# Statistics, Newton steps and three of four row tiles of the layer norm on GpSimd, in the first stage of a two-layer adaptive-norm kernel

## The chip, the cores and the metric

The kernel runs on one core of one Trainium2 chip, as one launch. The metric is device time in microseconds. A program's several executions are given by their median; the time of an execution is a little longer than the span that the profiler records from its first to its last instruction.

Engines are named as in the profile: PE (TensorE matrix products; PEld its weight loads), DVE (VectorE), ACT (ScalarE), POOL (GpSimd), SP (SyncE, here only issuing transfers). Each engine runs its own instructions in program order and waits on semaphores for the others.

## The reference

Two layers work on `x` of 4 batches x 1024 tokens x 256 features, all in float32. In each, `x` is normalised over its features, scaled and shifted by a modulation, sent through a mixing block, gated and added; the same again with a mixture of experts. The change concerns the two norms of the first layer:

```python
def _layernorm(x, axis=-1, eps=1e-05):
    m = jnp.mean(x, axis=axis, keepdims=True)
    v = jnp.var(x, axis=axis, keepdims=True)
    return (x - m) / jnp.sqrt(v + eps)
...
    x = L0_attn_hidden_states
    mod = (_silu(L0_c) @ L0_wmod).reshape(L0_c.shape[0], 6, 1, -1)
    sa, ca, ga, sb, cb, gb = (mod[:, 0], mod[:, 1], mod[:, 2], mod[:, 3], mod[:, 4], mod[:, 5])
...
    h = _layernorm(x, axis=-1) * (1 + ca) + sa
    x = x + ga * _L0_attn_ref(h, L0_attn_queries, L0_attn_combiners)
    h = _layernorm(x, axis=-1) * (1 + cb) + sb
    x = x + gb * _L0_ffn_ref(h, L0_ffn_W1, L0_ffn_b1, L0_ffn_W2, L0_ffn_b2, L0_ffn_Wr, L0_ffn_br)
...
```

`_L0_attn_ref` is attention without a softmax, in four head groups of 64, so it can be reordered: from the Gram matrix of the normalised tokens, a 64x64 product per group and the combiners, one matrix `md` is made per batch, and the block's output is `h` times `md`. `_L0_ffn_ref` picks the best two of eight experts per token by a router and runs each expert (256 to 1024 to 256). The second layer has a mixing block of gated products and again eight experts of which two are picked.

## The kernel before

**Stages.** The first stage (about the first 95 us) does the norms, the mixing block and the router of layer 0 and writes the normalised rows, with each token's expert numbers, to a table in memory (`h_rows`). Then come blocks of 128 token slots, gathered by expert, through the experts of layer 0; then layer 1. Only the first stage is touched by the change; from the first expert block on, each engine's program order is the same in both kernels.

**Tiles.** A row tile is 128 tokens x 256 features. A batch `b` has eight, taken in two groups `g` of four. For each batch there is a *first half* (`first_half`) and a *second half* (`second_half`), each with two groups, so `normalised` is called for 16 groups, 64 tiles in all.

**The norm of a group** (`normalised`). `stats` (L1097 to L1101) makes a tile's statistics on DVE: `bn_stats` gives six numbers per token (count, mean and sum of squared deviations of even and of odd elements), `bn_aggr` makes mean and variance of them, and after the fourth tile one operation adds epsilon (`ln_v`). `root` (L1105) takes the square root of the four variances on ACT. `newton` (L1109 to L1116) takes the reciprocal, one Newton step and `-mean * y` (`ln_m`) on DVE, each on 128x4 numbers. `scaled` writes the normalised tiles into `xn`: by `by_gpsimd`, tiles 0 and 1 of a group on POOL (L1126) and tiles 2 and 3 on ACT (L1128).

**Behind it.** `to_features` transposes the four tiles on PE (`pm_t`, L1168, 8 products), and ACT scales and shifts them while it takes them out of PSUM (L1173, `h1T` or `h2T`). It starts once all four tiles of the group are normalised. `to_tokens` transposes back (`pm_b`, L1195) and ACT copies the result over `xn` (L1200).

In a first half, PE then makes the Gram matrix from both groups (`pm_gram`, L1256), DVE copies its diagonal blocks (`gd`, L1267), PE multiplies by the combiners (`pm_t1`, L1289; the profile prints `pm_t`) and, after a copy by ACT (L1299), by the queries (`pm_m`, L1311), and DVE multiplies with the gate into `md` (L1324). In a second half, PE makes the block's output (`pm_o`, L1352), DVE adds it to `x` (L1362), two tiles at a time, the norm runs again, and PE makes the router's logits (`pm_e`, L194) and turns them to tokens (`pm_l`, L1404). DVE picks the best two experts in twelve operations (`route`, L420 to L446); SP stores rows and numbers (L1436, L1449). At the end of the stage `pm_turn` (L454 to L456) turns the choices of all tokens, and counting and the first gather by POOL (L353) follow.

**What sets the order.** The order on each engine is written by a list scheduler when the program is built (`Plan`): a piece of work is given by its engine, an assumed duration, the pieces that it follows, the buffers that it holds and a rank; at each planned moment the ready piece of the lowest rank goes to its engine. `FIRSTS` and `SECONDS` are the ranks of the batches' halves. `SPLIT` names the batch whose route is made in two halves of four tiles; the others are routed as eight. Where the plan leaves PE idle, pieces named `busy` (L1033, products of a constant that nobody reads) have been put, at planned times listed in the code and, 12 of them, after the split batch's logits:

```python
    for at in (15.6, 16.2, 16.8, 18.4, 19.0, 19.6, 21.2, 21.8, 23.4, 91.4, 98.9, 99.4):
        kept_busy(0.44, [], 40.0, at)
    for b in range(B):
        first_half(b, [5.5 + 5.0 * b, 8.0 + 5.0 * b])
        second_half(b)
```

**POOL's queue.** Before the norms it holds constants: identity, counters, masks. The mask `below16` (`affine_select`, L304) waits for `same16`, which DVE makes (L302), and behind it lie the clearings of `gd` and `md` and 24 small ones of `g_which` (L578). After the norms it issues the gathers and scatters of the expert blocks. DVE's queue holds, between the norms, the modulation's outputs (`modT`, L1063) and two rows of gates (`gate_of`, L338 to L342).

Of the kernel before, what the change touches and what calls it, by code (L numbers as in the profile page):

```python
# [8 lines left out]
F32 = mybir.dt.float32  # L9
# [3 lines left out]
ALU = mybir.AluOpType  # L13
# [6 lines left out]
P = 128  # L20
B, S, D = 4, 1024, 256
# [6 lines left out]
EPS = 1e-5  # L28
# [117 lines left out]
def adaln_d2_kernel(  # L146
# [20 lines left out]
    nc = tc.nc  # L167
# [36 lines left out]
    x_sb = const.tile([P, NC, B, D], F32, name="x_sb")  # L204
# [10 lines left out]
    pa = poolA.__enter__()  # L215
# [22 lines left out]
    for b in range(B):  # L238
        for g in range(2):
            cs = slice(4 * g, 4 * g + 4)  # L240
# [23 lines left out]
    rank = const.tile([P, E], F32, name="rank")  # L264
# [741 lines left out]
    for name, n in (("ga", 4 * B), ("gb", 3 * B)):  # L1006
        last = (blocks_of(n) - RARE) * P
# [17 lines left out]
    plan = Plan(p1=3, p2=2, pm=3, xn1=5, h1T=2, xn2=6, h2T=2, t1=1, le=2)  # L1025
    PE, ACT, DVE, POOL = "PE", "ACT", "DVE", "POOL"
    tiles = {}
# [56 lines left out]
        )  # L1084

    def by_gpsimd(k, b, g, i):
        return i < 2

    def normalised(b, cs, key, slot, after, rank, at=0.0):

        n = len(cs)

        def stats(c):
            if c == cs[0]:
                tiles["mv", key] = pa.tile([P, n, 2], F32, tag="ln_mv", name="ln_mv", bufs=6)
            st = pa.tile([P, 6], F32, tag="ln_st", name="ln_st", bufs=4)
            nc.vector.bn_stats(st, x_sb[:, c, b, :])  # L1097
            nc.vector.bn_aggr(tiles["mv", key][:, c - cs[0], :], st)
            if c == cs[-1]:
                v = tiles["v", key] = pa.tile([P, n], F32, tag="ln_v", name="ln_v", bufs=6)  # L1100
                nc.vector.tensor_scalar(v, tiles["mv", key][:, :, 1], EPS, None, ALU.add)  # L1101

        def root():
            y = tiles["y", key] = pa.tile([P, n], F32, tag="ln_y", name="ln_y", bufs=6)
            nc.scalar.activation(y, tiles["v", key], AF.Sqrt)  # L1105

        def newton():
            mv, v, y = tiles["mv", key], tiles["v", key], tiles["y", key]
            nc.vector.reciprocal(y, y)  # L1109

            t = pa.tile([P, n], F32, tag="ln_t", name="ln_t")
            nc.vector.scalar_tensor_tensor(t, y, -0.5, y, ALU.mult, ALU.mult)
            nc.vector.tensor_tensor(t, t, v, ALU.mult)
            nc.vector.scalar_tensor_tensor(y, t, 1.5, y, ALU.add, ALU.mult)
            m = tiles["m", key] = pa.tile([P, n], F32, tag="ln_m", name="ln_m", bufs=6)
            nc.vector.scalar_tensor_tensor(m, mv[:, :, 0], -1.0, y, ALU.mult, ALU.mult)  # L1116

        def scaled(i):
            if ("xn", key) not in tiles:
                tiles["xn", key] = pa.tile(  # L1120
                    [P, n, D], F32, tag=slot[0], name=slot[0], bufs=plan.room[slot[0]]
                )
            dst, src = tiles["xn", key][:, i, :], x_sb[:, cs[i], b, :]
            r, m = [tiles[q, key][:, i : i + 1] for q in ("y", "m")]
            if by_gpsimd(*key, i):
                nc.gpsimd.tensor_scalar(dst, src, r, m, ALU.mult, ALU.add)  # L1126
            else:
                nc.scalar.activation(dst, src, AF.Identity, bias=m, scale=r)  # L1128

        last = []  # L1130
        for i, c in enumerate(cs):
            last = [
                plan(
                    DVE,
                    0.54 if i < n - 1 else 0.71,
                    lambda c=c: stats(c),
                    after=[*last, *after(c)],
                    rank=rank,
                    at=at,
                )  # L1140
            ]
        r = plan(ACT, 0.22, root, after=last, rank=rank - 0.2)
        d = plan(DVE, 0.9, newton, after=[r], rank=rank - 0.2)
        done = []
        for i in sorted(range(n), key=lambda i: not by_gpsimd(*key, i)):
            pool = by_gpsimd(*key, i)
            done.append(
                plan(
                    POOL if pool else ACT,
                    0.8 if pool else 0.52,  # L1150
                    lambda i=i: scaled(i),
                    after=[d, *done[:1]],
                    holds=[slot],
                    rank=rank,
                )
            )
        return done
# [57 lines left out]

    of_batch = {}

    FIRSTS, SECONDS, SPLIT = [0, 1.3, 2.42, 2.65], [1.28, 4.7, 2.66, 4.55], 3

    def first_half(b, arrival):  # L1220

# [250 lines left out]
    q = plan("SP", 0.1, gates_out, after=rows_done, rank=-0.8, lag=2.2)  # L1472
# [15 lines left out]
    for half in range(2):  # L1488
# [15 lines left out]
        m = plan(PE, 0.3, turn, after=routes, holds=[ps], rank=rank_)  # L1504
# [38 lines left out]
    d = of_batch["turned"]  # L1543
    m = plan(PE, 0.2, lambda: g0.total_staged(ps_1), after=[d], holds=[ps], rank=-1.0)
# [183 lines left out]
    r, m0 = sought(0, [begun], -1.6)  # L1728
    r, m1 = sought(1, [r], -1.55)
# [11 lines left out]
    m = plan(PE, 0.4, lambda: g0.across(ps_1), after=[closed], holds=[ps], rank=-1.25)  # L1741
    d = plan(DVE, 1.6, lambda: g0.limits(pa), after=[m, bs], holds=[ps], rank=-1.0)
# [106 lines left out]
    def half_turned(j):  # L1849
# [40 lines left out]
        y=3,  # L1890
# [1159 lines left out]
```

## Time and profile before

| | us |
|---|---|
| runs, median of 13 (lowest, highest) | 1079.59 (1076.0, 1081.45) |
| the profiled execution | 1076.4 |
| its span, first to last instruction | 1074.7 |
| busy over the span: PE / PEld / DVE / ACT / POOL | 1037.6 / 802.0 / 602.4 / 396.1 / 425.6 |
| granted PE clock, mean | 0.995 |
| first transpose of the first norm begins (`pm_t`) | 11.91 |
| last `pm_l` of the stage ends | 92.04 |
| second `pm_turn` begins | 94.78 |
| first gather for an expert block (POOL) | 100.63 |

The columns of the views are as follows. A timeline row gives the start and the duration in us, the engine, the line, the operation, the tile written and those read, the shape, and how many instructions are merged. A row by stretches gives the stretch, its length, then the busy time of PE, PEld, DVE, ACT and POOL with the number of instructions, the granted clock, the share of the transfer engines and their rate. Matmuls are pipelined, so their busy time is modelled; the spacing from one start to the next says what one costs when nothing is waited for. On DVE a record starts a little before the record ahead of it ends, so there too the spacing counts. The profiled execution is one of the quicker ones, 3.2 us under the median.

### The profile page before, as it was taken

What the parts mean: (1) busy time and instruction counts of PE and PEld (TensorE: products, weight loads), DVE (VectorE), ACT (ScalarE), POOL (GpSimd) and SP (SyncE); (2) the same over time, 40 slices, a digit from 0 to 9 for tenths busy, and PEclk for the clock granted to TensorE, in tenths of its full rate; (3) what the DMA queues carried; (4) which work ended last, traced back from release to release, by engine and by line L of the source; (5) the groups of instructions that cost most, each with busy time, mean ns of one, the idle gap of its engine ahead of it and who ended that gap; (6) DMA issues with size and microseconds to landing.
All of it is one profiled execution on the core that took longest, in us unless ns stands there. A gap on an engine that the chain in (4) does not pass through costs nothing. (4 is left out here: it accounts for less than half of the span.)

```text
span 1074.7 us, 18875 instructions
## 1 busy us (share of the span) xinstructions
PE 1037.6 (97%) x6193; PEld 802.0 (75%) x6193; DVE 602.4 (56%) x2323; ACT 396.1 (37%) x1077; POOL 425.6 (40%) x509
## 2 busy tenths in 40 slices
PE   8998999999999999999999999999999999998993
PEld 5885899989989989989999465564656566646751
DVE  7997443232222232221175588878778726697767
ACT  5865332323232323232353333422224325342521
POOL 3211466545555655554453010110106321573644
PEclk9999999999999999999999999999999999999997
DMA  8605626675553725464171222221014322352534
GB/s 282 241 21 110 216 62 204 216 273 192 178 167 102 253 64 186 134 212 148 33 267 40 72 59 60 66 82 47 19 34 141 111 66 76 107 169 74 160 112 147
DMA packets 94255, 139.81 MB, mean 130 GB/s; under 512 B 31009, under 2 KB 69933, under 8 KB 89542
## 3 DMA queue, kind: packets, MB, share of 16 engines
q0 software_dynamic: 30080, 68.89, 20.2%
q1 hardware_dynamic: 62966, 68.04, 20.0%
q10 hardware_dynamic: 1104, 1.58, 0.4%
q8 instruction: 53, 0.87, 0.3%
q14 instruction: 52, 0.43, 0.1%
HBM read 202.22 MB, written 29.17 MB: 215 GB/s over the span
## 5 line engine op out<-in xcount | busy, mean ns | idle before, releaser
L1622 ACT ACTIVATE hid<-p_h,w 128x128 f32<-128x128 f32 x504 | 144.0, 369 | 301.4 <-issue 203.6
L1634 PE MATMUL p_y<-w,hid 128*128 128x256 f32 x1008 | 230.5, 382 | 0.6 <-DMA w<-in_W,g_wrow 0.6
L2430 PE MATMUL p_u<-hT,a 128*128 128x512 f32 x512 | 229.3, 595 | 1.3 <-ACTq L2395 0.9
L1634 PEld LDWEIGHTS p_y<-w,hid 128*128 128x128 f32 x1008 | 186.9, 190 | 24.6 <-issue 1.0
L2430 PEld LDWEIGHTS p_u<-hT,a 128*128 128x128 f32 x512 | 94.9, 190 | 103.1 <-issue 92.8
L1610 PEld LDWEIGHTS p_h<-xTq,w 128*128 128x128 f32 x1408 | 163.3, 192 | 1.7
L1610 PE MATMUL p_h<-xTq,w 128*128 128x128 f32 x1408 | 164.5, 275 | 0.0
L353 POOL DMA_INDIRECT w<-in_W,g_wrow x124 | 125.8, 1014 | 67.2 <-ACT hid L1622 42.7
L1645 DVE TENSOR_TENSOR y<-p_y,w 128x256 f32<-128x256 f32 x64 | 27.2, 425 | 193.6 <-PE p_y L1634 190.7
L914 POOL DMA_INDIRECT y<-y,g_dest x64 | 65.9, 1029 | 132.6 <-DVE y L1645 72.5
L2478 PE MATMUL p_f<-a,hf 128*128 128x256 f32 x512 | 116.9, 380 | 0.0
L2478 PEld LDWEIGHTS p_f<-a,hf 128*128 128x128 f32 x512 | 95.9, 190 | 18.7 <-issue 6.4
L2526 POOL TENSOR_TENSOR x_sb<-x_sb,step 128x256 f32<-128x256 f32 x32 | 24.6, 770 | 208.4 <-DVE step L2519 164.6
L860 DVE TENSOR_SCALAR_CACHE_REDUCE g_hits<-pm_counts,g_nth 128x128 f16<-128x128 f32 x68 | 23.7, 348 | 89.4 <-PE pm_counts L847 86.3
L1610 PE MATMUL p_h<-xT,w 128*128 128x128 f32 x608 | 71.3, 276 | 0.4 <-DVE xT L1567 0.4
L1610 PEld LDWEIGHTS p_h<-xT,w 128*128 128x128 f32 x608 | 70.3, 192 | 1.2 <-DVE xT L1567 0.6
L2442 ACT ACTIVATE hf<-p_u,decay 128x512 f32<-128x512 f32 x56 | 38.3, 685 | 77.2 <-PE p_u L2430 73.7
L2738 PE MATMUL p_e<-ew,xT 128*128 x256 | 64.9, 384 | 0.3 <-ACT y L2748 0.3
L2446 DVE SCALAR_TENSOR_TENSOR hf<-p_u,decay,hf 128x512 f32<-128x512 f32 x56 | 41.8, 747 | 22.1 <-PE p_u L2430 10.5
L2089 DVE TENSOR_TENSOR h<-h,mod 128x256 f32<-128x256 f32 x128 | 51.4, 423 | 4.1 <-ACT h L2079 2.1
L353 POOL DMA_INDIRECT xg<-ga_rows,ga_row x36 | 34.2, 950 | 45.6 <-DVE ga_row L869 13.5
L2738 PEld LDWEIGHTS p_e<-ew,xT 128*128 128x128 f32 x256 | 44.8, 190 | 8.6 <-issue 2.9
(420 smaller groups left out, 1340.5 us busy)
## 6 DMA issues: line engine op xcount, KB each, us to landing
yg<-y SPq DMA_DIRECT2D x32, 256.0 KB
xTq<-square SPq DMA_DIRECT2D x176, 32.0 KB
ew<-in_W SPq DMA_DIRECT2D x16, 288.0 KB
ga_y<-y SPq DMA_DIRECT2D x36, 128.0 KB
half<-in_W SPq DMA_DIRECT2D x16, 257.0 KB
x_sb<-in_x SPq DMA_DIRECT2D x8, 512.0 KB
h_rows<-xn SPq DMA_DIRECT2D x8, 512.0 KB
hT<-square SPq DMA_DIRECT2D x128, 32.0 KB
```

The source lines that it names most:

```text
L353: return nc.gpsimd.indirect_dma_start(out=dst, out_offset=None, in_=table, in_offset=bass.IndirectOffsetOnAxis(ap=index, axis=0), bounds_c ...
L914: nc.gpsimd.indirect_dma_start(out=table if parts == 1 else table.rearrange("r (i d) -> (r i) d", i=parts), out_offset=bass.IndirectOffset ...
L1610: nc.tensor.matmul(p1[:, i, :], lhsT=w1[:, k * H + m * P : k * H + (m + 1) * P], rhs=xT[k], start=(k == 0), stop=(k == KD - 1),)
L1622: nc.scalar.activation(hid[:, m, :], p1[:, i, :], AF.Relu, bias=w1buf[j % 2][:, KD * H + m : KD * H + m + 1],)
L1634: nc.tensor.matmul(p2, lhsT=hid[:, m, :], rhs=w2[:, m * D : (m + 1) * D], start=(m == 0), stop=(m == KH - 1),)
L1645: nc.vector.tensor_tensor(y, p2, w2buf[j % 2][:, KH * D :], ALU.add)
L2089: nc.vector.tensor_tensor(h, h, mods1[(sc, sh)[i]][:, b, :], (ALU.mult, ALU.add)[i])
L2430: nc.tensor.matmul(pu, lhsT=a[:, k, m * P : (m + 1) * P], rhs=made["n1", c, "hT"][:, k, :, :], start=(k == 0), stop=(k == KD - 1),)
L2442: nc.scalar.activation(made[key, m], made[key, m, 0], AF.Silu, scale=decays[c])
L2446: nc.vector.scalar_tensor_tensor(h, made[key, m, 1], decays[c], h, ALU.mult, ALU.mult)
L2478: nc.tensor.matmul(made[key, "p2", b], lhsT=made[key, m][:, b * P : (b + 1) * P], rhs=a1[:, m, :], start=(m == 0), stop=(m == KH - 1),)
L2738: nc.tensor.matmul(made[key, "p2"], lhsT=made[key, "xT"][:, k, :], rhs=ew_flat[:, bass.ds(made[key, "at"] + k * D, D)], start=(k == 0), st ...
```

## The change

The aggregation of the statistics leaves DVE. `stats` now only keeps the six numbers of four tiles side by side; a new piece `gathered` on POOL makes the four variances and twice the means of a group in seven operations on 128x4 numbers; the root stays on ACT; the reciprocal alone stays on DVE (`inverse`); the Newton step and `-mean * y` become six operations on POOL. `by_gpsimd` gives POOL three tiles of four. The planner's durations are changed with it, and `FIRSTS`, `SECONDS` and `SPLIT` get new values: the first halves of batches 0 and 1 come first, then the second half of 0, the first halves of 2 and 3, the second halves of 2, 3 and last 1, and batch 2 is the split one. (Before: the second half of 0 stood before the first half of 1 by rank, and the second halves ended with 3 and 1, with 3 split.) The list of `busy` pieces is unchanged.

```diff
@@ -1084,7 +1084,7 @@
         )
 
     def by_gpsimd(k, b, g, i):
-        return i < 2
+        return i < 3
 
     def normalised(b, cs, key, slot, after, rank, at=0.0):
 
@@ -1092,28 +1092,44 @@
 
         def stats(c):
             if c == cs[0]:
-                tiles["mv", key] = pa.tile([P, n, 2], F32, tag="ln_mv", name="ln_mv", bufs=6)
-            st = pa.tile([P, 6], F32, tag="ln_st", name="ln_st", bufs=4)
-            nc.vector.bn_stats(st, x_sb[:, c, b, :])
-            nc.vector.bn_aggr(tiles["mv", key][:, c - cs[0], :], st)
-            if c == cs[-1]:
-                v = tiles["v", key] = pa.tile([P, n], F32, tag="ln_v", name="ln_v", bufs=6)
-                nc.vector.tensor_scalar(v, tiles["mv", key][:, :, 1], EPS, None, ALU.add)
+                tiles["st", key] = pa.tile([P, n, 6], F32, tag="ln_st", name="ln_st", bufs=6)
+            nc.vector.bn_stats(tiles["st", key][:, c - cs[0], :], x_sb[:, c, b, :])
+
+        def gathered():
+            tiles["v", key], tiles["m", key] = [
+                pa.tile([P, n], F32, tag=f"ln_{x}", name=f"ln_{x}", bufs=6) for x in ("v", "m")
+            ]
+            g = nc.gpsimd
+            st, v = tiles["st", key], tiles["v", key]
+            d, q = [
+                pa.tile([P, n], F32, tag=f"ln_{x}", name=f"ln_{x}", bufs=2) for x in ("d", "q")
+            ]
+            g.tensor_tensor(d, st[:, :, 1], st[:, :, 4], ALU.subtract)
+            g.tensor_tensor(d, d, d, ALU.mult)
+            g.tensor_tensor(q, st[:, :, 2], st[:, :, 5], ALU.add)
+            g.tensor_scalar(d, d, 0.25, EPS, ALU.mult, ALU.add)
+            g.tensor_scalar(q, q, 1.0 / D, None, ALU.mult)
+            g.tensor_tensor(v, q, d, ALU.add)
+            m = tiles["m", key]
+            g.tensor_tensor(m, st[:, :, 1], st[:, :, 4], ALU.add)
 
         def root():
             y = tiles["y", key] = pa.tile([P, n], F32, tag="ln_y", name="ln_y", bufs=6)
             nc.scalar.activation(y, tiles["v", key], AF.Sqrt)
 
+        def inverse():
+            nc.vector.reciprocal(tiles["y", key], tiles["y", key])
+
         def newton():
-            mv, v, y = tiles["mv", key], tiles["v", key], tiles["y", key]
-            nc.vector.reciprocal(y, y)
-
-            t = pa.tile([P, n], F32, tag="ln_t", name="ln_t")
-            nc.vector.scalar_tensor_tensor(t, y, -0.5, y, ALU.mult, ALU.mult)
-            nc.vector.tensor_tensor(t, t, v, ALU.mult)
-            nc.vector.scalar_tensor_tensor(y, t, 1.5, y, ALU.add, ALU.mult)
-            m = tiles["m", key] = pa.tile([P, n], F32, tag="ln_m", name="ln_m", bufs=6)
-            nc.vector.scalar_tensor_tensor(m, mv[:, :, 0], -1.0, y, ALU.mult, ALU.mult)
+            v, y, m = tiles["v", key], tiles["y", key], tiles["m", key]
+            t = pa.tile([P, n], F32, tag="ln_t", name="ln_t", bufs=2)
+            g = nc.gpsimd
+            g.tensor_tensor(t, y, y, ALU.mult)
+            g.tensor_tensor(t, t, v, ALU.mult)
+            g.tensor_scalar(t, t, -0.5, 1.5, ALU.mult, ALU.add)
+            g.tensor_tensor(y, t, y, ALU.mult)
+            g.tensor_scalar(m, m, -0.5, None, ALU.mult)
+            g.tensor_tensor(m, m, y, ALU.mult)
 
         def scaled(i):
             if ("xn", key) not in tiles:
@@ -1132,22 +1148,24 @@
             last = [
                 plan(
                     DVE,
-                    0.54 if i < n - 1 else 0.71,
+                    0.42,
                     lambda c=c: stats(c),
                     after=[*last, *after(c)],
                     rank=rank,
                     at=at,
                 )
             ]
+        last = [plan(POOL, 0.75, gathered, after=last, rank=rank - 0.2)]
         r = plan(ACT, 0.22, root, after=last, rank=rank - 0.2)
-        d = plan(DVE, 0.9, newton, after=[r], rank=rank - 0.2)
+        r = plan(DVE, 0.2, inverse, after=[r], rank=rank - 0.2)
+        d = plan(POOL, 0.75, newton, after=[r], rank=rank - 0.2)
         done = []
         for i in sorted(range(n), key=lambda i: not by_gpsimd(*key, i)):
             pool = by_gpsimd(*key, i)
             done.append(
                 plan(
                     POOL if pool else ACT,
-                    0.8 if pool else 0.52,
+                    0.6 if pool else 0.52,
                     lambda i=i: scaled(i),
                     after=[d, *done[:1]],
                     holds=[slot],
@@ -1215,7 +1233,7 @@
 
     of_batch = {}
 
-    FIRSTS, SECONDS, SPLIT = [0, 1.3, 2.42, 2.65], [1.28, 4.7, 2.66, 4.55], 3
+    FIRSTS, SECONDS, SPLIT = [0.4, 0.69, 2.11, 2.24], [1.68, 3.87, 2.33, 2.69], 2
 
     def first_half(b, arrival):
```

## The prediction

> **What bounds the kernel now.** I read the stage table first, because the change lies in the first stage alone (program order on every engine is the same from the first expert block on). Two stretches, from the busy times by stretch (PE, PEld, DVE, ACT, POOL busy us, with instruction counts):
>
> ```profile
> 12.00:30.00 18.00, 16.88 (x176) 12.90 (x176) 16.43 (x70) 12.02 (x24) 3.67 (x7) 1.00 0.89 289
> 30.00:92.00 62.00, 58.74 (x719) 49.59 (x719) 55.62 (x225) 48.05 (x97) 13.10 (x24) 1.00 0.38 122
> ```
>
> The reader is to see that DVE is busy for 72 of these 80 us and POOL for 17, which invites the move, but also that PE is busy for 58.74 of the last 62. Whether that PE time is real I check by spacing, in the timeline:
>
> ```profile
> 36.20 2.09 PE L1256 MATMUL pm_gram<-xn 128*64 128x64 f32 x64
> ...
> 73.92 1.95 PE L1352 MATMUL pm_o<-md,h1T 128*128 128x128 f32 x16
> ```
>
> Back to back, a 128x128 matmul or transpose takes 1.95/16 = 0.122 us and a Gram matmul 2.09/64 = 0.033. The groups by line give 128 `pm_t` + 128 `pm_o` + 128 `pm_b` = 384 x 0.122 = 46.9; 256 Gram = 8.4; 128 router `pm_e` at 0.04 (0.64 for 16) = 5.1; 16 `pm_t1` at 0.257 = 4.1; 64 `pm_m` at 0.043 = 2.8; 8 `pm_l` at 0.11 = 0.9. That is 68.2 us that PE must do after the first transpose. Before, that transpose starts at 11.91 and the last `pm_l` ends at 92.04: 80.1 us, in which PE also does 16 `pm_modT` (1.9), one gate row (1.0) and 20 fillers of 0.213 (4.3). So it idles 4.7 us. PE is the second bound of the stage, right behind DVE, and gives a gain little room.
>
> **The change on DVE and ACT.** The norm's rows on DVE:
>
> ```profile
> 28.08 0.18 DVE L1098 BATCH_NORM_AGGREGATE ln_mv<-ln_st 128x2 f32<-128x6 f32 x1
> 28.18 0.39 DVE L1097 BATCH_NORM_STATS2 ln_st<-x_sb 128x6 f32<-128x256 f32 x1
> 28.61 0.18 DVE L1098 BATCH_NORM_AGGREGATE ln_mv<-ln_st 128x2 f32<-128x6 f32 x1
> 28.82 0.17 DVE L1101 TENSOR_SCALAR ln_v<-ln_mv 128x4 f32<-128x4 f32 x1
> 28.90 0.42 DVE L1097 BATCH_NORM_STATS2 ln_st<-x_sb 128x6 f32<-128x256 f32 x1
> ...
> 37.23 0.14 DVE L1109 RECIPROCAL ln_y<-ln_y 128x4 f32<-128x4 f32 x1
> ...
> 38.00 0.16 DVE L1116 SCALAR_TENSOR_TENSOR ln_m<-ln_mv,ln_y 128x4 f32<-128x4 f32 x1
> 38.08 0.42 DVE L1097 BATCH_NORM_STATS2 ln_st<-x_sb 128x6 f32<-128x256 f32 x1
> ```
>
> A stats-aggregate pair is spaced 0.53. Statistics without the aggregate were never back to back: between 0.32 (the overlap of about 0.08 that rows show) and 0.43 (none). So 64 pairs give back 0.10 to 0.21 each, 6 to 13 us; 16 `ln_v` 0.19 each (28.61 to 28.90, less 0.10), 3.0; and the Newton chain shrinks from 0.85 (37.23 to 38.08) to a reciprocal of 0.20, 16 x 0.65 = 10.4. DVE loses 20 to 27 us of 72. ACT loses 16 tiles of 0.545, 8.7 us of 60. Neither gain reaches the end by itself: PE and POOL come next. The statistics' six columns, now kept for four tiles, cost nothing, as no wait on a statistics buffer shows.
>
> **The change on POOL.** Each of 16 groups gains 7 small operations (aggregate), 6 (Newton) and one tile more. No small two-input operation on POOL is in the trace. The nearest rows:
>
> ```profile
> 2.73 0.18 POOL L289 CAST lane<-lane_i 128x1 f32<-128x1 int32 x1
> 2.85 0.20 POOL L289 CAST twice<-twice_i 128x32 f32<-128x32 int32 x1
> 3.01 0.28 POOL L289 CAST count<-count_i 128x128 f32<-128x128 int32 x1
> ...
> 31.06 0.16 DVE L1116 SCALAR_TENSOR_TENSOR ln_m<-ln_mv,ln_y 128x4 f32<-128x4 f32 x1
> ...
> 31.26 1.09 ACT L1128 ACTIVATE xn<-x_sb,ln_m,ln_y 128x256 f32<-128x256 f32 x2 [0.22 <-DVE ln_m L1116]
> 31.32 1.09 POOL L1126 TENSOR_SCALAR xn<-x_sb,ln_y,ln_m 128x256 f32<-128x256 f32 x2 [6.44 <-DVE ln_m L1116]
> ```
>
> Independent casts are 0.12 to 0.16 apart and take about 0.19. Woken by the same DVE result (ended 31.22), ACT starts 0.04 later and POOL 0.10 later. In the changed program's order, four of the seven and four of the six wait for POOL's own semaphore, so I take 0.19 + 0.10 = 0.29 from one dependent operation to the next and 0.14 between independent ones. Walking the two lists so, the aggregate holds POOL 1.29 us (the variance is out at 1.20), Newton 1.59, and three tiles at 0.545 take 1.64: g = 4.52 us a group, 72.3 in all. Lower end: all thirteen 0.12 apart, g = 3.2 (51 us). Upper end by the farthest row: a small operation as dear as a whole 128x256 tile, 13 x 0.545 + 1.64 = 8.7 a group, 140 us. I take 4.52, as a four-element operation is nearer to the 128x1 cast than to 256 elements; all thirteen in chain at 0.30 would make 5.5.
>
> A rule that speaks against the change stands in the Trainium skill, "GPSIMD Engine Reference", section "Engine selection": elementwise work belongs on VectorE, GpSimd being roughly twice as slow for two-input operations. As an estimate from that page, thirteen operations at twice DVE's spaced 0.20 would make a group 6.8 us, the queue 109 us and the kernel some 40 us slower; no row here shows that.
>
> **When POOL begins.** Its order puts the first aggregate behind `below16` and 24 memsets of `g_which`, which ended at 11.25 before; with six statistics ahead on DVE in place of five pairs I take 11.4. Then 1.20 to the variance, root and reciprocal (0.04 + 0.20 + 0.04 + 0.17 + 0.10), Newton 1.59, one tile, the second group's aggregate, two tiles: the first group is normalised at 17.7, where PE's first transposes started at 11.91. The reciprocal also sits in DVE's order where statistics of later tiles queue behind it, and the root on ACT has the drains of `pm_t` and `pm_b` behind it, whose buffers PE waits for: late POOL holds three queues. At this point DVE and ACT have slack, PE has not.
>
> **The sum by POOL's queue.** 11.4 + 72.3 = 83.7. Four groups (first, eleventh, thirteenth, fifteenth) have Newton straight behind their aggregate: 0.46 us of idling with ACT and DVE free, about 0.9 with half an instruction ahead on each: 3.6. The last first-half group (`xn_965`) must pass transposes, Gram, `t1`, `pm_m`, `pm_o` and the adds before group 13's statistics: 1.05 + 0.78 + 0.60 + 0.59 + 2.09 + 0.59 + 1.03 + 0.59 + 0.69 + 0.59 + 1.06 + 0.69 + 0.69 + 0.42 and a dozen hand-overs of 0.1 = 12.7, against 9.9 of POOL work between: 2.8. So the last tile is out at 90.1. Then the tail:
>
> ```profile
> 87.30 1.08 ACT L1128 ACTIVATE xn<-x_sb,ln_m,ln_y 128x256 f32<-128x256 f32 x2
> ...
> 91.71 0.33 PE L1404 MATMUL pm_l<-ident,le 128*128 128x128 f32 x1
> ...
> 92.08 0.19 DVE L420 TENSOR_REDUCE g_best<-pm_l 128x4 f32<-128x32 f32 x1
> ...
> 94.78 0.23 PE L454 MATMUL pm_turn<-ones,g_both 128*128 128x128 f16 x1 [0.20 <-DVE g_both L446]
> ```
>
> Last tile (88.38) to route 3.7, route to `pm_turn` 2.7. The last route now has eight tiles (batch 1 ends, SPLIT is 2): 3.2, as 86.12 to 89.31 shows; both turns come together, 0.3 more. 90.1 + 3.7 + 3.2 = 97.0, and 0.3: 2.5 us late.
>
> **The sum by PE.** 17.7 + 68.2 + 21 fillers (4.5) + 3 us of starving until batch 1 is normalised = 93.4, against 92.04: 1.4, with 0.8 for route and turns 2.2; if half of the old 4.7 of idling also stays, 4.6. Of 2.5, 2.2 and 4.6 I take 3.5, as two full queues that wait for each other lose more than either alone. On the profiled execution, 1076.4 (its span 1074.7 and 1.7 around it), that is 1079.9; it lay 3.2 under the median of the runs, so I forecast 1079.6 + 3.5 = **1083.1 us**. The stages behind follow one for one.
>
> Another rule would see more room: the Trainium skill, "Perfetto Trace Analysis", section "Identifying the Most-Contended Engine", calls the busy share of weight loads the good metric and the matmul share a bad one. PEld is busy 49.59 of 62, so by that rule, as an estimate from the page, 12 us could go and the kernel reach 1067. The start-to-start spacing says 3.
>
> **Rivals.** A, *PE packs*: POOL's small operations cost the lower end, in the first 25 us and all along. Then the first group is out at 16.0 (1.29 and 1.59 become 0.84 and 0.72), POOL never decides, and PE ends at 16.0 + 68.2 + 4.5 = 88.7 if it never idles otherwise: 2.5 faster after 0.8 for route and turns; at the spacing of weight loads (1.86 us for 16, 0.116) 384 x 0.006 = 2.3 more. 1074.8 to 1077.1, say 1076. For it: DVE 90% busy now. Against: eight waits a group. It decides from g under about 3.6. B, *no change*: g near 4.1, where POOL's sum is 11.4 + 65.6 + 6.4 + 7.2 = 90.6 and only PE's late start is left, against what it packs: within 2 us, 1079.6. C, *the chain is dearer*: g = 5.5, 11.4 + 88 + 6.4 + 7.2 = 113, 18 us late, 1098. Against it: casts of 0.18. D, the code does not do what it says: program order shows the operations on POOL, so no.
>
> **Chances.** Forecast (1081.8 to 1089) 0.47, A 0.25, B 0.17, C and what lies between 0.11. A measurement of this kernel can tell 0.2%, 2.2 us. Faster 0.25, same 0.17, slower 0.58. Range 1074.5 to 1095: A's bound below; above, most of the way to C, with the 8.7 end left out.
>
> **What would show it.** POOL busy about 65 to 75 us of the first 100, small operations 0.25 to 0.30 apart in chains; first `pm_t` at 17 to 18; DVE waiting for ACT's root; `pm_turn` at 97 to 99. If `pm_turn` comes before 92, either POOL's operations were cheaper or my PE count is too high.

## The result and the profile after

The changed kernel took 1095.78 us (median of 8 runs, 1093.59 to 1097.69) against 1079.49 of the kernel before (36 runs, 1076.0 to 1081.46): a ratio of 1.0154, 95% interval 1.0142 to 1.0165, 16.3 us slower. I had forecast 3.5 slower, and a range up to 1095. The direction was right; the size was out by more than a factor of four, and the time lies just outside the range. The profiled execution took 1093.6 us with a span of 1091.6, 16.9 over that of before (1074.7).

The same two stretches as in the prediction, and the end of the stage behind them (busy us of PE, PEld, DVE, ACT, POOL with counts, then the granted PE clock, DMA share and GB/s):

```profile
12.00:30.00 18.00, 12.91 (x118) 9.25 (x119) 11.22 (x39) 7.54 (x16) 14.01 (x64) 0.81 0.89 287
30.00:92.00 62.00, 55.71 (x638) 47.74 (x637) 32.28 (x93) 34.20 (x68) 45.01 (x172) 0.94 0.23 87
92.00:108.00 16.00, 14.47 (x152) 10.08 (x151) 9.96 (x48) 12.69 (x25) 6.38 (x22) 1.00 0.67 157
```

DVE went from 72 to 43.5 us in the first two rows, and POOL from 17 to 59. Over the whole stage (12 to 95 us before, 12 to 108 now) DVE has 74.5 and 53.5 us: 21 less, inside the 20 to 27 that I had worked out. But PE, the second bound, went from 16.88 + 58.74 to 12.91 + 55.71, and part of that at a lower clock: it issued 756 matmuls by 92 us where it had issued 895. No engine is full, and the stage is 13 us longer. So this is a loss by waiting. What waited is in the list of waits between 12 and 108 us (engine, line, what it waited for: us in total, times, longest):

```profile
ACT ln_y L1118 <- POOL ln_v L1112: 23.1, 12, 6.5
DVE ln_y L1121 <- ACT ln_y L1118: 22.4, 10, 5.0
PEld pm_t L1186 <- POOL xn L1142: 9.3, 12, 2.6
ACT xn L1144 <- POOL ln_m L1132: 9.2, 6, 2.5
POOL ln_d L1107 <- DVE ln_st L1096: 8.2, 1, 8.2
```

The first two rows are new and belong to the round trip: ACT stands at the root for POOL's variance, DVE stands at the reciprocal for ACT's root. The last is the other way round, one stall of 8.2 us in which POOL itself has nothing to do.

Was POOL dearer than I had worked out? Its timeline (start, duration, engine, line, operation), one aggregate and one Newton list:

```profile
22.27 0.20 POOL L1107 TENSOR_TENSOR ln_d<-ln_st 128x4 f32<-128x4 f32 x1
22.54 0.20 POOL L1108 TENSOR_TENSOR ln_d<-ln_d 128x4 f32<-128x4 f32 x1
22.69 0.20 POOL L1109 TENSOR_TENSOR ln_q<-ln_st 128x4 f32<-128x4 f32 x1
22.99 0.20 POOL L1110 TENSOR_SCALAR ln_d<-ln_d 128x4 f32<-128x4 f32 x1
23.27 0.22 POOL L1111 TENSOR_SCALAR ln_q<-ln_q 128x4 f32<-128x4 f32 x1
...
23.88 0.20 POOL L1107 TENSOR_TENSOR ln_d<-ln_st 128x4 f32<-128x4 f32 x1
...
43.72 0.20 POOL L1127 TENSOR_TENSOR ln_t<-ln_y 128x4 f32<-128x4 f32 x1
...
45.04 0.20 POOL L1132 TENSOR_TENSOR ln_m<-ln_m,ln_y 128x4 f32<-128x4 f32 x1
45.19 0.20 POOL L1127 TENSOR_TENSOR ln_t<-ln_y 128x4 f32<-128x4 f32 x1
```

A dependent operation follows after 0.27 to 0.28 (L1107 to L1108), an independent one after 0.15 (L1108 to L1109); an aggregate takes 1.61 from start to start (22.27 to 23.88), a Newton list 1.47 (43.72 to 45.19), and 48 tiles lie 0.54 apart. A group is 1.61 + 1.47 + 1.62 = 4.7 us, where I had 4.52. The sum was right to 4%, its parts less so: the aggregate takes 1.61 where I had 1.29, as L1110 and L1111 too start 0.28 to 0.30 after the operation ahead of them, and the Newton list 1.47 (1.63 where a tile follows it, 18.88 to 20.51) where I had 1.59.

How a late POOL list holds three queues is seen best between 40 and 51 us:

```profile
48.49 0.20 POOL L1112 TENSOR_TENSOR ln_v<-ln_q,ln_d 128x4 f32<-128x4 f32 x1
48.64 0.20 POOL L1114 TENSOR_TENSOR ln_m<-ln_st 128x4 f32<-128x4 f32 x1
48.72 0.20 ACT L1118 ACTIVATE ln_y<-ln_v 128x4 f32<-128x4 f32 x1 [6.49 <-POOL ln_v L1112]
48.83 0.56 POOL L1142 TENSOR_SCALAR xn<-x_sb,ln_y,ln_m 128x256 f32<-128x256 f32 x1
48.83 0.57 ACT L1317 COPY t<-pm_t 128x512 f32<-128x512 f32 x1
48.96 0.18 DVE L1121 RECIPROCAL ln_y<-ln_y 128x4 f32<-128x4 f32 x1 [5.00 <-ACT ln_y L1118]
49.17 0.69 DVE L1380 TENSOR_TENSOR x_sb<-x_sb,pm_o 128x512 f32<-128x512 f32 x1
...
49.45 1.12 PE L1329 MATMUL pm_m<-t,qT 128*64 128x64 f32 x16 [3.29 <-ACT t L1317]
```

The planner put the root of one group ahead of the copy of `t` of batch 1 on ACT, and the reciprocal ahead of the adds on DVE. POOL's variance came 6.5 us after ACT stood ready; the copy, whose input PE had finished at 45.3, had to stand behind it, and `pm_m`, the heart of batch 1, stood on PE for the copy. Those are three queues held by one late list. Batch 1 pays (PE's `pm_o` show that the second halves run in the order 0, 1, 2, 3, although batch 1 has the last rank), as PE's and POOL's timelines show further on:

```profile
50.51 5.21 PE L1186 MATMUL pm_t<-ident,xn 128*128 128x128 f32 x20
...
57.94 1.06 PE L1370 MATMUL pm_o<-md,h1T 128*128 128x128 f32 x8
...
63.54 1.06 PE L1370 MATMUL pm_o<-md,h1T 128*128 128x128 f32 x8
```

```profile
68.85 0.20 POOL L1107 TENSOR_TENSOR ln_d<-ln_st 128x4 f32<-128x4 f32 x1 [8.19 <-DVE ln_st L1096]
```

Behind `pm_m` come twenty transposes and batch 0's router; only then `pm_o` of batch 1, whose second part is out at 64.6, and the add and the statistics after it. The add begins at 65.81 only, behind batch 0's route on DVE (62.87 to 65.89), and the statistics have the `gd` copies and another add between them. The eleventh group, the first half of batch 1's second norm, needs them: POOL, which was late at 48, is starved from 60.66 to 68.85.

And the tail, PE's last rows of the stage:

```profile
104.35 0.33 PE L1422 MATMUL pm_l<-ident,le 128*128 128x128 f32 x1
...
107.80 0.23 PE L454 MATMUL pm_turn<-ones,g_both 128*128 128x128 f16 x1
...
107.98 0.22 PE L454 MATMUL pm_turn<-ones,g_both 128*128 128x128 f16 x1
```

The last `pm_turn` is at 107.98, before it was at 94.78: 13.2 of the 16.9 are in the stage. The first gather on POOL starts at 115.15 where it was at 100.63: 14.5. The way from the last turn to the gather is 7.2 in place of 5.9. That the two turns now come together does not explain it: in numbers 6 and 7 below they do too, and it is 3.5 and 3.6. In the changed kernel the row numbers for the gather are ready at 111.87 (`g_row`), and the transfer engines are busy at a share of 0.72 or more up to 112 us with the last rows for the table, which SP sent off from 105.18 on. The gather reads that table; that it waited for those rows is likely, but no run shows it.

### The profile page after: what moved, and what is told of

It reads as the page before. It is cut to its first block, busy times and chain, and to the rows that moved or that the text cites. A ratio compares the mean times of both kernels' runs of the same rounds, so it can differ in the third digit from the quotient of the medians.

```text
span 1091.6 us, 18922 instructions
## 1 busy us (share of the span) xinstructions
PE 1042.5 (96%) x6193; PEld 805.9 (74%) x6193; DVE 578.9 (53%) x2179; ACT 388.7 (36%) x1061; POOL 473.1 (43%) x733
## 5 line engine op out<-in xcount | busy, mean ns | idle before, releaser
L353 POOL DMA_INDIRECT xg<-ga_rows,ga_row x36 | 34.4, 957 | 46.2 <-DVE ga_row L869 16.9
```

The source lines that it names most:

```text
L353: return nc.gpsimd.indirect_dma_start(out=dst, out_offset=None, in_=table, in_offset=bass.IndirectOffsetOnAxis(ap=index, axis=0), bounds_c ...
```

## Experiments

Three theories. CHAIN: POOL's queue, 4.7 us a group, is simply too long and its round trips too slow. ORDER: the planner lays out a fixed order on every engine by the prices it is told, and was told 0.75 for each of the two lists, half of the 1.61 and 1.47 that they take; so operations that wait for POOL are put too early in in-order queues. The three new lists of ranks belong to that order. CLOCK: PE's granted clock falls when it starves, and matmuls take twice as long.

The chip of the first four ran the kernel before at 1098 to 1116 us, with much scatter; there the traces' first stage decides, and the ratios only loosely.

**1. The ranks and the split of before, in the changed kernel.**

```
-    FIRSTS, SECONDS, SPLIT = [0.4, 0.69, 2.11, 2.24], [1.68, 3.87, 2.33, 2.69], 2
+    FIRSTS, SECONDS, SPLIT = [0, 1.3, 2.42, 2.65], [1.28, 4.7, 2.66, 4.55], 3
```

> The changed kernel with the three lists of ranks and the split of before (FIRSTS, SECONDS, SPLIT); the work on each engine stays that of the changed kernel. Theory CHAIN (thirteen small POOL operations a group, 4.7 us a group by the trace, make every normalised group late): the order matters little, 1092 to 1099 us. Theory ORDER (the new ranks and the wait of both turns for the last route cost it: +1.5 us from turn to first gather, and the 8.2 us in which POOL starves at 60.7 to 68.9): 1086 us or less. Theory CLOCK (PE starves, its granted clock falls to 0.5 to 0.73 for some us, and matmuls take twice as long): says nothing of this run.

1.0203 (1.0129 to 1.0277); last `pm_turn` at 117.39, 9.4 later still than in the changed kernel. Neither theory had that: CHAIN said "little", ORDER said better. The new ranks are not to blame by themselves; with these prices and this division of the work they do better than the old ones. But order alone is worth 9 us, which speaks against CHAIN as the whole cause.

**2. The planner told what the trace shows.**

```
-        last = [plan(POOL, 0.75, gathered, ...
+        last = [plan(POOL, 1.6, gathered, ...
-        d = plan(POOL, 0.75, newton, ...
+        d = plan(POOL, 1.5, newton, ...
-                    0.6 if pool else 0.52,
+                    0.55 if pool else 0.52,
```

> The changed kernel, its planner told what the trace shows: 1.60 for the aggregate and 1.50 for the Newton list where it had 0.75 each, 0.55 for a tile where it had 0.60. ORDER (the static order is laid out for lists of half their length, so every in-order queue waits for POOL at the wrong place): the POOL idle of 8.2 us shrinks below 3 and the time falls to 1084 to 1089 us. CHAIN: POOL still has 75 us of work and the same round trips: 1092 to 1098 us.

1.0043 (1.0007 to 1.0079); last `pm_turn` at 102.87, first gather at 108.24, 6.9 earlier than in the changed kernel. Every instruction is the same, only their order differs. POOL's longest stall fell as ORDER said:

```profile
72.79 0.20 POOL L1107 TENSOR_TENSOR ln_d<-ln_st 128x4 f32<-128x4 f32 x1 [2.06 <-DVE ln_st L1096]
```

**3. Fillers on PE where it starves.** 42 matmuls more, before the transposes of the first two groups and before batch 1's `pm_m`; the other engines' order is untouched.

```
+    WARM = {(1, 0, 0): 4.5, (1, 0, 1): 1.9}
...
             def mm(k=k):
+                if k == 0 and key in WARM:
+                    busy(WARM[key])
...
         def head_m():
+            if b == 1:
+                busy(3.2)
```

> The changed kernel with 42 fillers more on PE (0.213 us each, 9 us in all), put in PE's order where the trace has it idle for POOL or ACT: 20 before the first group's transposes, 8 before the second's, 14 before batch 1's pm_m. Order on every other engine unchanged. CLOCK (the low clock after these idles costs 1.2 us on each of the first two groups, 0.5 on the next drain and 2.8 on twenty transposes at 50.5, 5 to 6 us in all, on the path): 1089 to 1092 us, granted clock 1.00 throughout the first 60 us. CHAIN: POOL sets the pace, the slow transposes hide in its lateness: 1094.5 to 1097 us though the clock is full.

1.0103 (1.0028 to 1.0177) on the noisy chip; the trace decides. First the changed kernel, then this one, stretches with PE busy first and the granted clock third from the end:

```profile
20.00:24.00 4.00, 3.12 (x13) 2.13 (x12) 3.93 (x12) 2.78 (x5) 3.47 (x13) 0.50 0.38 94
48.00:52.00 4.00, 2.55 (x21) 1.83 (x21) 2.93 (x8) 1.62 (x4) 3.40 (x13) 0.57 0.02 6
```

```profile
20.00:30.00 10.00, 9.66 (x110) 6.73 (x108) 7.56 (x24) 6.32 (x13) 8.24 (x38) 1.00 0.76 256
50.00:60.00 10.00, 8.17 (x69) 6.15 (x69) 3.13 (x9) 7.75 (x15) 8.91 (x25) 1.00 0.15 52
```

The clock stays at 1.00 all through the stage, the transposes at 50 us are fast again, and the last `pm_turn` comes at 107.00 in place of 107.98, the first gather at 114.83 in place of 115.15. So in this stage the low clock costs 0.3 to 1.0 us, not 5: PE only waited longer for POOL. Even that is no more than two executions of the changed kernel differ by in these marks (108.84 and 114.38 in number 5). CLOCK falls as the cause of the late turn. Behind the turn the clock does fall in this run (0.50 from 112 to 114 us), and the first `pm_x` still comes 3.0 us after the gather.

**4. POOL's lists shortened.** The Newton step's own four operations are left out.

```
-            g.tensor_tensor(t, y, y, ALU.mult)
-            g.tensor_tensor(t, t, v, ALU.mult)
-            g.tensor_scalar(t, t, -0.5, 1.5, ALU.mult, ALU.add)
-            g.tensor_tensor(y, t, y, ALU.mult)
```

> The changed kernel without the Newton step itself (four of the six operations of that list; the reciprocal of the root is used as it is, so this kernel leaves out the correction of the root). A group on POOL falls from 4.7 to about 3.6 us, 16 x 1.1 = 17 us less in POOL's queue. CHAIN: 10 to 14 us come back, 1081 to 1086 us. ORDER: no more than a third of it, 1090 us or more. My prediction set the point from which POOL stops deciding at 3.6 a group, so by it this run lies within 3 us of the kernel before.

1.0017 (0.9986 to 1.0047); last `pm_turn` at 96.46, first gather at 104.12. 16 x 1.0 us less on POOL bring 11.5 at the turn and 11.0 at the gather. That is what CHAIN said. But it shortens a list to 0.46 that was planned at 0.75, so it also changes the misfit; it can't tell the two apart by itself. The long stall of POOL is still there, as long as before and only 8.8 us earlier:

```profile
60.09 0.20 POOL L1107 TENSOR_TENSOR ln_d<-ln_st 128x4 f32<-128x4 f32 x1 [8.66 <-DVE ln_st L1096]
```

So the stall by itself is not the loss: with shorter lists ahead of it and behind it, a run that has it ends within about 2 us of the kernel before.

**5. The changed kernel again**, as the control of the next chip, on which all runs are close (the kernel before 1075.89 to 1077.90).

> The changed kernel again, as the control of this call, as the kernel before ran from 1098 to 1116 us on the chip of the last call. Every theory: a ratio of 1.010 to 1.020, the last pm_turn at 106 to 109 us in the trace.

1.0162 (1.0145 to 1.0179), last `pm_turn` at 108.84, first gather at 114.38. Against the first profile of the same kernel these marks moved by 0.9 later and 0.8 earlier, so differences of 1 us between two traces say nothing.

**6 and 7. One list back on DVE.** Number 6 restores `bn_aggr` and the sum with the epsilon; number 7 the Newton list:

```
-        d = plan(POOL, 0.75, newton, after=[r], rank=rank - 0.2)
+        d = plan(DVE, 0.7, newton, after=[r], rank=rank - 0.2)
...
+            nc.vector.scalar_tensor_tensor(t, y, -0.5, y, ALU.mult, ALU.mult)
+            nc.vector.tensor_tensor(t, t, v, ALU.mult)
+            nc.vector.scalar_tensor_tensor(y, t, 1.5, y, ALU.add, ALU.mult)
+            nc.vector.scalar_tensor_tensor(m, m, -0.5, y, ALU.mult, ALU.mult)
```

> The changed kernel with the aggregate back on DVE (bn_aggr for each tile and one sum with the epsilon); Newton list and third tile stay on POOL: 3.1 us a group in place of 4.7. CHAIN: POOL's queue loses 25 us, more than the 17.6 that brought the last pm_turn from 108.0 to 96.5 without the Newton step, so PE or DVE sets the end: last pm_turn 93 to 97, ratio 0.998 to 1.004. ORDER (only the misfit of planned and real length matters, here 1.45 against 0.75 for one list still): 98 to 102, 1.004 to 1.008.

1.0103 (1.0087 to 1.012), last `pm_turn` at 104.24.

> The changed kernel with the Newton list back on DVE (four operations there); the aggregate and the third tile stay on POOL, 3.25 us a group. CHAIN: 93 to 98 for the last pm_turn, ratio 0.998 to 1.004. ORDER (the aggregate of 1.60 is still planned at 0.75): 98 to 103. If the aggregate costs more than the Newton list because statistics must cross to POOL and back through ACT and DVE before any tile, this run ends later than the one with the aggregate on DVE.

1.0089 (1.0072 to 1.0106), last `pm_turn` at 104.02. CHAIN's 93 to 98 is missed by both, though they took 25 and 23 us off POOL, more than number 4; POOL is idle for half of the stage in them and the end still comes 9 us late. The two lists cost much the same. What both keep are the new ranks, and one list that is planned at half its length.

**8. The new ranks and split alone, in the kernel before.**

> The kernel before with the three lists of ranks and the split of the changed kernel, nothing else. CHAIN: the order is worth little, the last pm_turn within 2.5 us of 94.8, ratio 0.998 to 1.003. ORDER (the new ranks themselves cost it): last pm_turn at 100 or later, ratio 1.005 or more.

1.0080 (1.0063 to 1.0097): 7.8 us slower with not one instruction on another engine; last `pm_turn` at 101.61. ORDER. The ranks that suit one division of the work spoil another, in both directions (number 1 is the other one, though number 14 shows that the planner's prices do most of it there).

**9. The whole change in an order of its own**: true prices as in number 2, and ranks chosen anew for these prices.

```
+    FIRSTS, SECONDS, SPLIT = [0.72, 1.12, 0, 2.57], [0.81, 2.3, 4.5, 2.34], 2
```

> The whole change, its planner told 1.60, 1.50 and 0.55 for the POOL pieces, and three lists of ranks chosen anew for these prices (SPLIT stays 2). CHAIN: POOL has 75 us of work behind 11.8 and six more before the route, so the last pm_turn cannot come before 11.8 + 75.2 + 3.6 + 7 = 97.6; with any starving it lies at 99 to 103 and the ratio at 1.004 to 1.009. ORDER (an order that fits the true lengths takes the loss away): 95 to 98, ratio 0.999 to 1.003.

1.0068 (1.005 to 1.0087): 7.8 us slower, where the changed kernel was 17.0 slower in number 5. Last `pm_turn` at 99.80, inside what CHAIN said. The same stretch as above, 30 to 92 us:

```profile
30.00:92.00 62.00, 60.84 (x739) 51.63 (x736) 37.93 (x120) 41.90 (x82) 50.27 (x191) 1.00 0.29 103
```

PE is busy for 60.84 of 62 at full clock, against 55.71 in the changed kernel: the order had kept it waiting. POOL's last tile is out at 92.7, against 99.4. What is left is at both ends. From 12 to 30 us PE issues 106 matmuls instead of the 176 of before, as the first transpose waits for POOL until 17.80. And at the seam to the expert blocks the last turn stands 1.82 us for the eight-tile route, and PE's rows behind it show

```profile
99.62 0.23 PE L454 MATMUL pm_turn<-ones,g_both 128*128 128x128 f16 x1 [1.82 <-DVE g_both L446]
...
103.86 6.28 PE L1541 MATMUL pm_mod<-wmod,sT 128*4 128x256 f32 x20
110.07 0.51 PE L1580 MATMUL pm_x<-ident,xg 128*128 128x128 f32 x2
```

with a granted clock of 0.59 and 0.56 from 100 to 108 us. Twenty `pm_mod` take 6.28 us, 4.48 in the changed kernel, and the first `pm_x` stands behind them: 5.0 us after the gather has started, 2.9 before. The same is seen in numbers 6, 7 and 8: the twenty take 6.13, 5.57 and 5.30 us, and the first `pm_x` comes 6.4, 5.6 and 5.1 us after the gather. So 2 to 3.5 us of what these runs lose are lost behind the gather, and not by the order of the stage. The profiled execution of number 9 is also the slowest of its four (1087.19 against a median of 1085.21).

**10, 11 and 12. Half of the change, with its own order.** Number 10 is number 7 and number 11 is number 6, each with true prices and ranks chosen anew; number 12 is number 10 with other ranks and the split on batch 3.

```
number 10
+    FIRSTS, SECONDS, SPLIT = [1.11, 1.28, 2.19, 1.9], [4.01, 5.69, 2.52, 2.51], 2
number 11
+    FIRSTS, SECONDS, SPLIT = [1.04, 1.16, 3.76, 1.39], [1.0, 4.2, 2.58, 3.89], 2
number 12
+    FIRSTS, SECONDS, SPLIT = [0.18, 0.1, 1.54, 2.62], [0.12, 3.16, 2.66, 3.0], 3
```

> Aggregate and third tile on POOL (3.25 us a group, 52 us in all, planned at 1.60 and 0.55), Newton on DVE, three lists of ranks chosen anew for it, SPLIT 2. CHAIN and ORDER together: neither POOL nor DVE is full, PE's 68 us and its first transpose at 16 to 18 set the end: last pm_turn 91 to 95, ratio 0.995 to 1.000. If the ranks were not what held the run with Newton on DVE at 104.0, it stays above 100 and at 1.005 or more.

1.0023 (1.001 to 1.0036), last `pm_turn` at 95.75, first gather at 101.81: a little later than I expected, but 8.3 us earlier at the turn than number 7.

> Newton and third tile on POOL (planned at 1.50 and 0.55), aggregate on DVE, ranks chosen anew for it, SPLIT 2. CHAIN and ORDER together: last pm_turn 92 to 97, ratio 0.996 to 1.002. If the ranks did not matter, 104 and 1.010 as before.

0.9988 (0.9977 to 0.9999), last `pm_turn` at 92.56, first gather at 97.11, 3.5 ahead of the kernel before; 11.7 earlier at the turn than number 6.

> As the run with Newton on DVE and its own order, with other ranks, in which batch 3's second half is the split one (SPLIT 3, as in the kernel before): two turns apart from each other and a last route of four tiles in place of eight. If the two turns in one and the eight-tile route cost 2 us (7.35 against 5.85 from turn to gather), this run is 1 to 3 us earlier at the first gather than its sister though the last tile comes no sooner: ratio 0.994 to 1.000.

0.9992 (0.9981 to 1.0004), last `pm_turn` at 94.00, first gather at 98.37: 3.4 earlier at the gather than number 10, although the last tile is out at 86.5 against 86.1. Its two turns are 2.35 apart. But in number 10 they are 2.42 apart too, so what I expected the two-in-one turns to cost is not what this pair tells apart, and the price of the eight-tile route stays open: the ranks differ as well.

**13. The shortened lists of number 4 in an order of their own** (1.60, 0.46 and 0.55; the Newton step's correction is left out).

> The changed kernel without the four operations of the Newton step (the correction of the root is left out), 3.7 us a group on POOL, its planner told 1.60, 0.46 and 0.55, ranks chosen anew for it, SPLIT 3. With the order out of the way, what is left of the loss is POOL's length: the whole change in an own order ended at 99.8 with 4.7 a group; 1.0 x 16 = 16 us less in POOL's queue puts PE or DVE in its place. CHAIN: last pm_turn 91 to 95 and a ratio of 0.996 to 1.001. If what remained at 99.8 was not POOL's length but the first group's lateness (17.8 against 11.9 for the first transpose), it gains the Newton step's 1.0 us alone: 98 to 99, ratio 1.005.

1.0009 (1.0 to 1.0018), last `pm_turn` at 97.08, first gather at 100.41. By time and gather this is what CHAIN said: with 1.0 us a group off POOL's queue the 7.8 us that number 9 still lost are down to about 1. But the ranks and the split differ from number 9 as well, so the gain is not shown to be POOL's length alone. By the turn it is 2 us later than I said; the way from there to the gather is 3.3 us here, 5.9 before, so the turn is the poorer mark of the two. The first transpose is still at 17.43, so lateness of the first group alone is not what costs the 7.8. Some 2 us of the gain are at the seam, which keeps its clock at 1.00 here, as the row of the twenty shows:

```profile
99.27 4.48 PE L1536 MATMUL pm_mod<-wmod,sT 128*4 128x256 f32 x20
```

**14. True prices with the ranks of before.**

> The whole change with the three lists of ranks and the split of before, its planner told the true 1.60, 1.50 and 0.55. Of the misfit, this gives the prices back and leaves the ranks to the kernel before. If the prices are what misfits, last pm_turn at 101 to 106, near the 102.9 of the changed ranks with true prices and far from the 117.4 of the old ranks with 0.75: ratio 1.006 to 1.012. If the ranks are, it stays above 110 and at 1.015 or more.

1.0072 (1.0058 to 1.0087), last `pm_turn` at 104.18, first gather at 107.30. With the old ranks and 0.75 it was 1.0203 and 120.58 (number 1). With the ranks held fixed, the prices in the planner bring the turn 13.2 us forward, and with them right the choice between these two sets of ranks matters little in time (1.0072 old, 1.0068 own).

**15. Number 11 again, in five rounds.**

> The run with the aggregate on DVE and its own order again, in five rounds, as the one version that came out ahead of both kernels (0.9988, 0.9977 to 0.9999). If its last pm_turn at 92.6 against 94.8 is real, 0.997 to 0.9995; if not, the interval reaches over 1.

0.9984 (0.9975 to 0.9993): 1.5 us faster than the kernel before, and some 18 faster than the changed one. Its stretch from 30 to 92 us, where the kernel before had PE 58.74, DVE 55.62 and POOL 13.10:

```profile
30.00:92.00 62.00, 61.56 (x745) 52.59 (x744) 49.19 (x184) 44.33 (x89) 31.70 (x101) 1.00 0.38 128
```

PE is full, fillers included. This version keeps the aggregate on DVE, moves the Newton list and the third tile, and tells the planner 1.50 and 0.55. The kernel before with ranks chosen anew was not run, so it is not shown that the 1.5 us come from the move and not from the new ranks.

The runs in one view (us; last `pm_turn` and first gather from the trace):

| run | last turn | gather | ratio |
|---|---|---|---|
| before | 94.8 | 100.6 | 1 |
| changed kernel | 108.0 | 115.2 | 1.0154 |
| 2: true prices | 102.9 | 108.2 | 1.0043 (noisy chip) |
| 14: true prices, old ranks | 104.2 | 107.3 | 1.0072 |
| 9: true prices, own ranks | 99.8 | 105.1 | 1.0068 |
| 13: 1.0 us a group less, own ranks, split 3 | 97.1 | 100.4 | 1.0009 |
| 8: new ranks, nothing moved | 101.6 | 105.5 | 1.0080 |
| 15: aggregate on DVE, own ranks | 93.1 | 97.9 | 0.9984 |

## Why the prediction was wrong

**What held.** The price of a group (4.52 said, 4.7 measured), built from a cast of 0.18 and a wake-up of 0.10, was right to 4%, partly because an aggregate that was too cheap and a Newton list that was too dear made up for each other. POOL is busy for 71.4 of the first 100 us, inside the 65 to 75 that I named. POOL's start was nearly right (11.4 said, 11.79 measured), and the first group was 1.2 us later than said (normalised at 17.7 said, POOL's last tile out at 18.9). The last route does have eight tiles, though it is batch 3's and not batch 1's as I wrote. The relief of DVE was there. Statistics without the aggregate run back to back at 2.68/8 = 0.335, between the 0.32 and 0.43 I gave:

```profile
21.92 2.68 DVE L1096 BATCH_NORM_STATS2 ln_st<-x_sb 128x6 f32<-128x256 f32 x8
```

PE's 68 us and its 0.122 a matmul held too: once the order let it, PE was full (60.84 and 61.56 of 62), and the best version gained 1.5 us, not the 12 that a busy share of weight loads would promise.

**What failed.** It is the step "The sum by POOL's queue", and in it the idles: "about 0.9 ... 3.6" and "9.9 of POOL work between: 2.8". From the first aggregate at 11.79 to the last tile at 99.43 are 87.6 us, of which 16 x 4.7 = 75.2 are work: 12.4 us beyond the work, not 6.4. One stall of 8.2 makes most of it, at group 11, not at group 13 where I had put 2.8. The whole difference to my turn at 97.3 is then: start 0.4, price 0.18 x 16 = 2.9, idling 6.0, last tile to turn 8.55 instead of 7.2, 1.4; together 10.7, and 97.3 + 10.7 = 108.0.

**Why the idles were wrong.** I walked POOL's order as if it had been laid out for the lengths that I had just worked out. It was not: the diff that I read says `plan(POOL, 0.75, gathered` and `plan(POOL, 0.75, newton`, and I had 1.29 and 1.59 on the same page. An order laid out for half of the length puts root and reciprocal of each group 0.9 us too early (1.61 less 0.75) and its first tile 1.6 (0.72 more for Newton), in three in-order queues, and the error adds up over the groups that follow each other on POOL. I named the risk ("late POOL holds three queues") and gave it no more than the step from 2.5 to 3.5 us. The runs price it: with true prices and the same instructions, the gather comes 6.9 to 10.1 us earlier (numbers 2, 14 and 9), and the time falls from 17.0 us over the kernel before (number 5) to 7.6 and 7.8 (numbers 14 and 9). In the order of number 9 my sum does hold: with 4.7 in place of 4.52 it gives 97.3 + 2.9 = 100.2, and the turn came at 99.80. Its terms are near too (start 12.1 for 11.4, idles 5.4 for 6.4, last tile to turn 7.1 for 7.2), but the longest stall is 1.1 us, not the 2.8 that I had placed before group 13, so that the idles fit is partly luck.

**What the rest is.** Of 17 us, 9 go when the order is mended and 8 are left (number 9); with 16 us less on POOL, other ranks and another split those 8 are down to about 1 (number 13), so most of them probably follow from POOL's length, but that was not isolated. The two causes are no simple sum either: shorter lists in the old order alone brought 11.5 us at the turn (number 4), with the long stall still there. The forecast's 3.5, chosen between 2.2 and 4.6, is that same term, and it was short too: the turn came 5.0 late instead of 2.5, the price of a group being 0.18 higher, and the trace shows another 2.1 behind the gather, where PE had starved before the turn and ran the twenty `pm_mod` at a lower clock. I had no term for that. It changes from one execution to the next: the changed kernel ran these twenty in 4.48 us in its first profile and in 5.56 in number 5.

**"The stages behind follow one for one"** was nearly so: turn +13.2, gather +14.5, end +16.9 in the changed kernel. The 1.3 between turn and gather is there in the trace. The 2.4 behind the gather is within what one execution differs from the next (before: 1076.0 to 1081.46). Where PE starves at the seam, as in number 9, it does not hold.

**The rivals.** C, "the chain is dearer", named 1098 and the measurement is near, but by another mechanism: its price of 5.5 a group is not there, 4.7 is. A needed 3.6 a group; numbers 4 and 13 had 3.7 and came within about 2 us of the kernel before, but number 6, at 3.1 a group in the changed kernel's order, still lost 11 us. So there is no such point by the price alone: it holds only where the order fits. The rule I had weighed against the change (Trainium skill, "GPSIMD Engine Reference", "Engine selection": twice as slow for two inputs, by which a group would cost 6.8) is not what the rows show: 0.20 for a small operation, 0.15 apart if independent and 0.28 if not.

## What to carry to other kernels

When a static planner orders the work, a diff that moves an operation has two prices: what it takes, and what the planner is told; put them side by side before anything else, since a list planned at half its length stalls every in-order queue that has been lined up behind it. Ranks chosen for one division of the work need not carry over to another: the new ones alone made the kernel before 7.8 us slower, though its work had not moved at all. A wait of 8 us on the new engine may be a sign that its consumers were held up earlier, so look at what stood behind the late result in the other queues; and don't take the longest wait for the loss, as number 4 kept it and lost little.

## Unexpected of the hardware

The granted PE clock, 1.00 all through the first stage before, fell twice after PE had starved. After the idles up to 18.4 us it was 0.73 and then 0.50, and after the 3.29 us at 46.2 it was 0.57 and 0.58 for two stretches of 4 us, in which the twenty transposes took 5.21: 0.26 each instead of 0.122. An idle of 1.3 us (95.0 to 96.4) left the clock at 1.00. By the Trainium skill, "TensorE: Matmul & The Clock Gate", section "What's actually happening", the clock is either full or half, and goes to half after an idle window of about 3.4 us. The stall of 3.29 us agrees with that; the length of a single idle does not settle it, though. In number 9 the clock was at 0.50 from 102 to 106 us, and the longest single idle before was 1.82 us, followed by short matmuls and small gaps. The runs add where it matters: within the stage the clock fell where PE waited for POOL anyway, and keeping it at 1.00 there brought at most 1.0 us (number 3); at the seam of number 9, where PE's own queue stood before the first `pm_x`, it went with 6.28 us for work that takes 4.48.
